# Splitting expert weights in one ScalarE copy and one GpSimd subtraction a block, with no VectorE mask

## The chip, the cores and the metric

The kernel runs on one core of one Trainium2 chip. The metric is device time in microseconds, the median of several executions. The engines are called PE (TensorE), DVE (VectorE), ACT (ScalarE), POOL (GpSimd) and SP (SyncE, which issues most DMAs here).

## The reference, cut to what matters

The input `x` has shape (32, 64, 1024). Two layers are run, each a conditioned chain of four small convolutions (same, upsample, same, downsample) followed by a feed-forward part, with a residual. The first layer's feed-forward part is a gated low-rank mixture of 64 experts:

```python
scores = xf @ Wr.T
top_vals, top_idx = jax.lax.top_k(scores, TOPK)        # 16 of 64
gates = jax.nn.softmax(top_vals, axis=-1)
G = jnp.zeros((N, K)).at[jnp.arange(N)[:, None], top_idx].set(gates)
h = jnp.einsum('nd,krd->nkr', xf, A)                   # 64 experts, rank 16, d = 1024
out = jnp.einsum('nkr,kdr->nd', h * G[:, :, None], B)
```

The second layer's is a product with int4 weights that are unpacked first. The change touches the preparation of `A` (with `Wr` in front of it) and `B` alone.

## The kernel before, in words

Samples are worked on in 16 pairs; a pair's tokens fill the 128 partitions. There are three phases, each a loop over the pairs: `layer0` (convolutions and the product with `[Wr | A]`, then gating, the result stored to DRAM), `layer0b` (that result transposed and multiplied by `B`, residual added), and `layer1` (convolutions and the unpacked weights).

Products with weights are made in float32r, in three parts. Each token tile is split into an upper half `th` and a lower half `tl` (scaled by RADIX = 4096), and a third tile `td` is the difference of the two. Each weight block of 128 rows has three planes to match: plane 0 is the upper half, plane 1 the remainder, plane 2 the crossed form, plane 0 − RADIX × plane 1. `product` runs all blocks with the planes 0 and 1 (`Q`) into one bank and plane 2 (`D`) into another. The blocks are `wa0` to `wa7` (1088 columns: 64 of `Wr`, 1024 of `A`) and `wb0` to `wb7` (1024 columns of `B`).

Making the planes is `split_weights`. Before the change it goes through a block in chunks of 512 columns (1088 gives 512, 512 and 64). For each chunk, `high` on DVE (line 150) clears the low 12 bits by two shifts, into a tile of the ring `hi`, which has three buffers and is shared with the splits of tokens (line 921) and with the unpacking of int4 weights (line 441). POOL subtracts that tile from the raw weights into plane 1 (line 383), and ACT copies it into plane 0 (line 384). Then DVE makes plane 2 for the whole block (`crossed_weights`, line 391).

While the blocks are still being split, the first two pairs (`WHOLE`) of `layer0` and of `layer0b` work on the raw weights in plain float32, without planes. Raw `A` blocks arrive by DMA in the rooms of later blocks: `w5` holds raw blocks 2 to 4, `w6` raw 5, 0 and 1, `w7` raw 6, and a tile named `kept` raw 7. So a block can be written only when the raw blocks that lie in its room have been read for the last time. Raw `B` blocks lie in the buffer `cv`; `wb0` to `wb7` take the rooms of `wa0` to `wa7`.

The code is written in program order, and a planner then orders the instructions of each engine by readiness and by its own estimate of times, so that an instruction can run well before its place in the text. `with tc.issue_after(ins)` sets a limit to that: each instruction that the block emits on the engine of `ins` is queued behind `ins`; instructions on other engines are not bound by it. The splits are spread over the start of `layer0` in this way: `wa3` before the loop (behind `done["c"]`, a PE instruction); `wa0` and `wa1` behind `xe` (a DVE instruction of `ends`); `wa4` behind `s2` (DVE); `wa2` behind `re` (an ACT copy); `wa5` and `wa6` during pair 1, `wa6`'s crossed form behind `lo`; `wa7` behind the gates of pair 1 (DVE), its crossed form behind `lo` too. `wb0` to `wb3` are emitted in pair 0 of `layer0b`, `wb4` to `wb7` in pair 1.

Beside the splits, in pair 0 of `layer0`, runs `ends(0, …)`: a row of small operations that make the outermost values of all samples, with PE matmuls `ye` (line 502), `ue` (521), `ve` (546) and `re` (559), and DVE work between them (`scaled`, lines 474 and 477, and `blur`, lines 530 to 532). Other names that come up: `rest` with the matmuls at 838, 847, 856 and 879 and the DVE additions 869, 870 and 887; the sums of composed weights on POOL (646, 652); second differences on POOL (726, 734); gating on POOL (1009); convolution matmuls 760, 761, 772, 777; the joining of products with the residual on DVE (1129, 1130); `tdx` and `tdh`, the tokens' difference on POOL (939).

Of the kernel before, what the change touches and what calls it, by code (L numbers as in the profile page):

```python
# [8 lines left out]
F32 = mybir.dt.float32  # L9
# [3 lines left out]
ALU = mybir.AluOpType  # L13
# [12 lines left out]
H = 512  # L26
# [37 lines left out]
def adaln_ffn_kernel(ctx: ExitStack, tc: tile.TileContext, t, out: bass.AP):  # L64
    nc = tc.nc
# [77 lines left out]
    def block(k, shape, dt, name):  # L143

        return wts.tile(shape, dt, tag=f"w{k}", name=name)

    def high(src, name):

        v = wk.tile([P, H], I32, tag="hi", name=name, bufs=3)[:, : src.shape[1]]
        nc.vector.tensor_scalar(  # L150
            v, src.bitcast(I32), BITS, BITS, ALU.logical_shift_right, ALU.logical_shift_left
        )
        return v.bitcast(F32)
# [222 lines left out]
    def split_weights(raw, w, ks, into, name, crossed=True):  # L376

        for k in ks:
            ws = block(k, [P, 3, w], F32R, f"{name}{k}")
            for c in range(0, w, H):  # L380
                cs = slice(c, min(c + H, w))
                h = high(raw[k][:, cs], f"{name}h{k}_{c}")
                nc.gpsimd.tensor_tensor(ws[:, 1, cs], raw[k][:, cs], h, ALU.subtract)
                nc.scalar.copy(ws[:, 0, cs], h)  # L384
            into[k] = ws
            if crossed:
                crossed_weights(into, k)

    def crossed_weights(into, k):
        ws = into[k]  # L390
        nc.vector.scalar_tensor_tensor(  # L391
            ws[:, 2], ws[:, 1], -RADIX, ws[:, 0], ALU.mult, ALU.add
        )
# [915 lines left out]
    def split_behind(v, k):  # L1309
        with tc.issue_after(done[v].ins):  # L1310
            split_weights(araw, AW, (k,), wa, "wa")
# [33 lines left out]
    with tc.issue_after(done["c"].ins):  # L1345
        split_weights(araw, AW, (3,), wa, "wa")
# [9 lines left out]
    for k in range(NP):  # L1356
# [31 lines left out]
        if k == 1:  # L1388
            beside[1] += [(split_weights, araw, AW, (5,), wa, "wa", False)]
            beside[2] += [(crossed_weights, wa, 5)]  # L1390
            beside[3] += [(weights, k + 2), (split_weights, araw, AW, (6,), wa, "wa", False)]
# [161 lines left out]
```

## Time and profile before

| | |
|---|---|
| median of 3 runs | 893.77 us (892.96 to 894.99) |
| the profiled execution | 891.84 us, span 889.8 us |
| mean granted clock of PE | 0.997 |
| line 150, masks of weights: 24 for `wa`, 16 for `wb` | 128x512 mean 0.56 us beside `araw`, 0.89 us beside `cv` |
| line 383, subtractions of the split | 128x512 mean 1.43 us (`wa`), 1.58 us (`wb`) |
| line 384, copies of the split | 128x512 mean 0.62 us |
| line 391, crossed form | 128x1088 mean 1.34 us, 128x1024 mean 1.97 us |

A profile is one execution; its times are microseconds from the start of the span. An instruction group is given as line, engine, operation, output and inputs, shape, count; what stands in brackets behind a piece of the timeline is how long the engine had been idle and what ended that. The chain of waits is followed back from the last instruction. In windows, the busy time of each engine in a stretch is followed by the granted clock of PE, the DMA share and GB/s.

### The profile page before, as it was taken

What the parts mean: (1) busy time and instruction counts of PE and PEld (TensorE: products, weight loads), DVE (VectorE), ACT (ScalarE), POOL (GpSimd) and SP (SyncE); (2) the same over time, 40 slices, a digit from 0 to 9 for tenths busy, and PEclk for the clock granted to TensorE, in tenths of its full rate; (3) what the DMA queues carried; (4) which work ended last, traced back from release to release, by engine and by line L of the source; (5) the groups of instructions that cost most, each with busy time, mean ns of one, the idle gap of its engine ahead of it and who ended that gap; (6) DMA issues with size and microseconds to landing.
All of it is one profiled execution on the core that took longest, in us unless ns stands there. A gap on an engine that the chain in (4) does not pass through costs nothing.

```text
span 889.8 us, 14891 instructions
## 1 busy us (share of the span) xinstructions
PE 861.4 (97%) x5023; PEld 773.3 (87%) x5023; DVE 723.9 (81%) x1461; ACT 355.6 (40%) x817; POOL 531.8 (60%) x745
## 2 busy tenths in 40 slices
PE   6989989999999999999999999999999999999997
PEld 5877789999999999994688888888899999999996
DVE  5565888888888888768996666669999999999996
ACT  6444444444444444433432221247333433443340
POOL 7335754666666665556572222343887888888884
PEclk9999999999999999999999999999999999999999
DMA  8531213222222222344465765566433234324311
GB/s 244 147 73 51 52 62 86 83 81 82 78 76 74 74 76 72 119 166 155 140 213 193 229 195 175 189 194 190 146 107 110 87 118 118 110 96 140 107 66 72
DMA packets 49739, 107.83 MB, mean 121 GB/s; under 512 B 13764, under 2 KB 22400, under 8 KB 49664
## 3 DMA queue, kind: packets, MB, share of 16 engines
q1 hardware_dynamic: 48704, 105.90, 37.9%
q10 hardware_dynamic: 960, 0.99, 0.5%
q8 instruction: 40, 0.66, 0.3%
q14 instruction: 35, 0.29, 0.1%
HBM read 69.00 MB, written 37.86 MB: 120 GB/s over the span
## 4 chain that ended last, share of the span: by engine, by line
PE 41%; DVE 8%; POOL 2%; issue 2%; ACT 0%; DVEq 0%; POOLq 0%
PE o L959 16%; PE q L1211 11%; PE f L623 3%; PE r L879 2%; PE c L777 2%; PE r L838 1%; PE ht L1085 1%; PE r L847 1%; PE c L772 1%; PE g L600 1%; DVE cv L720 1%; DVE cv L778 1%; DVE r L888 1%; DVE rt L870 1%; DVE nib L443 1%
## 5 line engine op out<-in xcount | busy, mean ns | idle before, releaser
L720 DVE TENSOR_TENSOR cv<-cv 128x257 f32<-128x257 f32 x120 | 106.7, 921 | 1.1 <-ACT cv L762 0.9
L734 POOL TENSOR_TENSOR cv<-cv 128x256 f32<-128x256 f32 x120 | 77.5, 646 | 28.8 <-DVE cv L720 15.9
L726 POOL TENSOR_TENSOR cv<-cv 128x128 f32<-128x128 f32 x100 | 38.8, 409 | 68.1 <-DVE su L1002 55.1
L1211 PE MATMUL q<-wq,thx 128*128 128x342 f32 x384 | 73.1, 332 | 3.5 <-ACT thx L917 2.9
L1211 PE MATMUL q<-wq,tlx 128*128 128x342 f32 x384 | 72.3, 330 | 0.0
L959 PE MATMUL h<-wa,tdx 128*128 128x352 f32 (+1 forms) x336 | 72.0, 350 | 0.2 <-DVE wa L391 0.2
L623 PE MATMUL f<-gs,iw 128*128 128x128 f32 (+1 forms) x384 | 68.2, 327 | 0.0
L623 PEld LDWEIGHTS f<-gs,iw 128*128 128x128 f32 x384 | 61.9, 191 | 5.5 <-POOL iw L260 0.2
L1211 PEld LDWEIGHTS q<-wq,thx 128*128 128x128 f32 x384 | 60.4, 189 | 5.5 <-ACT thx L917 4.0
L959 PE MATMUL h<-wa,thx 128*128 128x352 f32 (+1 forms) x336 | 64.8, 334 | 0.0
L774 ACT ACTIVATE yt<-c,be,al 128x257 f32<-128x257 f32 x56 | 31.7, 566 | 80.4 <-PE c L772 80.3
L879 PE MATMUL r<-cv 128*128 128x128 f32 x480 | 63.4, 275 | 0.0
L1211 PEld LDWEIGHTS q<-wq,tlx 128*128 128x128 f32 x384 | 61.6, 189 | 0.8
L959 PE MATMUL h<-wa,tlx 128*128 128x352 f32 (+1 forms) x336 | 62.3, 327 | 0.0
L959 PE MATMUL o<-wb,thh 128*128 128x512 f32 x224 | 59.8, 401 | 1.6 <-ACT wb L384 1.6
L939 POOL TENSOR_TENSOR tdx<-thx,tlx 128x1024 fp32r<-128x1024 f32 x14 | 35.4, 2532 | 43.0 <-ACT tlx L931 34.7
L959 PEld LDWEIGHTS h<-wa,tdx 128*128 128x128 f32 x336 | 56.8, 188 | 2.4 <-DVE wa L391 0.5
L879 PEld LDWEIGHTS r<-cv 128*128 128x128 f32 x480 | 58.4, 191 | 0.0
L646 POOL TENSOR_TENSOR cv<-cv 128x256 f32<-128x256 f32 x60 | 50.2, 836 | 13.2 <-ACT cv L641 13.1
L959 PE MATMUL o<-wb,tlh 128*128 128x512 f32 x224 | 58.0, 397 | 0.0
L638 ACT COPY cv<-f 128x256 f32<-128x256 f32 x64 | 23.9, 374 | 85.3 <-PE f L623 71.8
L980 ACT ACTIVATE hs<-h,outd 128x368 f32<-128x368 f32 (+1 forms) x42 | 23.7, 564 | 83.4 <-PE h L959 83.1
(318 smaller groups left out, 2266.9 us busy)
## 6 DMA issues: line engine op xcount, KB each, us to landing
cv<-in_x_dram SPq DMA_DIRECT2D x60, 256.0 KB
cv<-x1e SPq DMA_DIRECT2D x64, 192.5 KB
x1e<-dd SPq DMA_DIRECT2D x16, 514.0 KB
hgd<-hs SPq DMA_DIRECT2D x16, 512.0 KB
hg<-hgd SPq DMA_DIRECT2D x16, 512.0 KB
x1d<-x SPq DMA_DIRECT2D x16, 512.0 KB
xb<-x1d SPq DMA_DIRECT2D x16, 512.0 KB
out_dram<-o SPq DMA_DIRECT2D x15, 512.0 KB
```

Source lines behind the costliest of these rows:

```text
L623: done["f"] = nc.tensor.matmul(pv[:, n : n + 2 - k], iw[:, e].rearrange("p a b -> p (a b)"), v, start=(m == 0), stop=(m == len(steps) - 1) ...
L638: nc.scalar.copy(f8[:, 0::2], pv[:, :, h])
L646: nc.gpsimd.tensor_tensor(f[:, 4 * P : 6 * P].rearrange("p (a b) -> p a b", b=P), v[:, :, 0], v[:, :, 1], ALU.add,)
L720: nc.vector.tensor_tensor(d[:, k], yo[:, k : k + HQ], yb, ALU.subtract)
L726: nc.gpsimd.tensor_tensor(y[:, YB + k * P : YB + (k + 1) * P], y[:, 2 * k : 2 * k + 2 * P - 1 : 2], y[:, 1 : 2 * P : 2], ALU.subtract,)
L734: nc.gpsimd.tensor_tensor(e[:, :, k], d[:, :, 2 * k : 2 * k + HQ - 2 : 2], d[:, :, 1 : HQ - 1 : 2], ALU.subtract,)
L774: nc.scalar.activation(yt, mid, AF.Identity, bias=be0[:, n : n + 1], scale=a)
L879: done["r"] = nc.tensor.matmul(ps[:, j * P : (j + 1) * P], y[:, YE + (2 * q + k) * P : YE + (2 * q + k + 1) * P], w(q + 2 * k), start=True ...
L939: done["td"] = nc.gpsimd.tensor_tensor(*(v.rearrange("p a b -> p (a b)") for v in (td, *toks[key])), ALU.subtract)
L959: nc.tensor.matmul(banks[l == 2], toks[key][l][:, order(k)], w[:, cols], start=(k == first and l != 1), stop=(k == last and l in (2, min(n ...
L980: nc.scalar.activation(dst, qd[0], AF.Copy, scale=outd[:, 0, p : p + 1])
L1211: nc.tensor.matmul(ps, half[:, k], wq[at(k)][:, c * QC : (c + 1) * QC], start=(k == 0 and j == 0), stop=(k == NC - 1 and j == 1),)
```

## The change

The loop over chunks goes. ACT copies a whole raw block into plane 0, which is of the type float32r, in one operation; that copy rounds to the nearest value of the type, where the mask cut the low bits off. POOL subtracts plane 0, read as float32, from the raw block into plane 1, also in one operation a block. DVE's part in `split_weights` is the crossed form alone. The guards of the callers stand as they were.

```diff
         for k in ks:
             ws = block(k, [P, 3, w], F32R, f"{name}{k}")
-            for c in range(0, w, H):
-                cs = slice(c, min(c + H, w))
-                h = high(raw[k][:, cs], f"{name}h{k}_{c}")
-                nc.gpsimd.tensor_tensor(ws[:, 1, cs], raw[k][:, cs], h, ALU.subtract)
-                nc.scalar.copy(ws[:, 0, cs], h)
+            nc.scalar.copy(ws[:, 0], raw[k][:, :w])
+            nc.gpsimd.tensor_tensor(
+                ws[:, 1], raw[k][:, :w], ws[:, 0].bitcast(F32), ALU.subtract
+            )
             into[k] = ws
             if crossed:
                 crossed_weights(into, k)
```

## The prediction

> **What bounds the kernel now.** I read the page first. Its part 1:
>
> ```profile
> span 889.8 us, 14891 instructions
> ...
> PE 861.4 (97%) x5023; PEld 773.3 (87%) x5023; DVE 723.9 (81%) x1461; ACT 355.6 (40%) x817; POOL 531.8 (60%) x745
> ```
>
> TensorE (PE) is busy 97% of the span; only 889.8 − 861.4 = 28.4 us of it are gaps. Work taken off VectorE (DVE) is worth nothing unless it closes one of those gaps, so the second view is what PE waited for:
>
> ```profile
> PE ve L546 <- DVE room L532: 3.0, 1, 3.0
> ...
> PE c L777 <- DVE rt L870: 2.0, 3, 1.0
> PE o L959 <- ACT wb L384: 1.6, 2, 0.9
> ...
> PE c L777 <- DVE tlx L923: 1.0, 2, 0.6
> PE re L559 <- DVE room L532: 0.6, 1, 0.6
> ```
>
> The columns are total, times, longest. L384 is the split's own copy. Expert-weight splits run in two stretches only, 25 to 116 us (wa, factor A) and 383 to 436 us (wb, factor B). Inside those, the waits that touch the split are: 3.0 (L546), 0.6 (L559), 1.0 and 0.6 (L777, at 110.0 and 122.0 us; the third L777 wait is later), 0.2 (a crossed block of wa) and 1.6 (wb). Third view, the timeline at 41 to 50 us, shows what the 3.0 is:
>
> ```profile
> 41.17 0.93 PE L521 MATMUL ue<-room,cu 128*128 128x160 f32 x6
> ...
> 41.70 2.06 DVE L150 TENSOR_SCALAR wah<-araw 128x512 int32<-128x512 int32 x2 [1.38 <-ACT wa L384]
> ...
> 43.69 1.28 DVE L391 SCALAR_TENSOR_TENSOR wa<-wa 128x1088 fp32r<-128x1088 f32 x1
> ...
> 44.89 1.26 DVE L150 TENSOR_SCALAR wah<-araw 128x64 int32<-128x64 int32 x1
> ...
> 46.08 0.44 DVE L474 TENSOR_TENSOR room<-ue,alp 128x288 f32<-128x288 f32 x1
> ...
> 46.59 1.29 DVE L391 SCALAR_TENSOR_TENSOR wa<-wa 128x1088 fp32r<-128x1088 f32 x1
> ...
> 47.80 0.46 DVE L477 TENSOR_TENSOR room<-room,bep 128x288 f32<-128x288 f32 x1
> ...
> 49.55 0.73 PE L546 MATMUL ve<-room,cw 128*128 128x192 f32 x3 [3.01 <-DVE room L532]
> ```
>
> The bank `ue` is full at 42.1, but DVE reads it (L474) only at 46.08: masks (L150) and a crossed block (L391) stand in front, and a mask of 64 columns takes 1.26 because GpSimd (POOL) is subtracting beside it (shortest L150 here: 0.18). The whole row of small edge operations then ends late, and PE, out of other work at 46.54, waits. Fourth, the chain of waits in the wb stretch:
>
> ```profile
> 426.54 1.07 DVE x L1130
> 427.61 2.02 DVE wbh L150 x3
> 429.65 0.63 ACT wb L384
> 430.32 11.17 PE o L959 x41
> ```
>
> PE is held by a mask on DVE, that DVE reached only after L1130, and by the ACT copy behind it; ACT itself had been idle 7.19 us until 427.69. Fifth, the windows there (PE, PEld, DVE, ACT, POOL busy, then the granted clock):
>
> ```profile
> 429.00:430.00 1.00, 0.41 (x1) 0.09 (x1) 1.00 (x2) 0.72 (x2) 1.00 (x2) 1.00 0.52 184
> 430.00:431.00 1.00, 0.68 (x2) 0.58 (x3) 1.00 (x2) 0.27 (x1) 1.00 (x2) 0.67 0.48 127
> 431.00:432.00 1.00, 1.00 (x4) 0.81 (x3) 1.00 (x2) 0.94 (x4) 1.00 (x1) 0.50 0.95 385
> ```
>
> PE idles 0.73 + 0.59 + 0.32 = 1.64 us from 428 to 431, and right behind it the clock is 0.67, 0.50, 0.50, 0.63 for four microseconds, 1.70 us of full-speed work lost. The same matmul costs 3.32/8 = 0.415 us there and 1.98/8 = 0.248 at 435.9.
>
> **The change, part by part.** *Removed from DVE:* 40 masks (L150). wa: 14 of 512 columns busy 7.8, 7 of 64 columns 4.0, the three of `kept` 2.1; wb: 16 busy 13.5. Together 27.4 us, nearly all with PE busy beside it. *ACT:* 40 copies busy 9.5 + 1.9 + 9.4 = 20.8 become 16. The nearest row is L931, 128x1024 into fp32r at 1.056; with L384 (512: 0.616) the slope gives 1.11 for 1088. So 8×1.11 + 8×1.06 = 17.3. *POOL:* 40 subtractions busy about 50.5 become 16; nearest row L939, 128x1024 at 2.42 to 2.53, hence about 2.6 for 1088 and some 40 in all (quiet halves, 1.27 each, give the same per column: the saving is contention). *Crossed form:* 16 operations, unchanged.
>
> *The new wait.* POOL now waits for the ACT copy of the whole block, where it waited for a DVE mask of half a block. From raw block to crossed block: 1.11 + 2.6 + 1.28 = 5.0 us; before, undisturbed, 0.42 + 2×1.27 + 0.3 + 1.28 = 4.5. So 0.5 more per block, covered wherever blocks are made ahead of their use. Queued behind POOL's wait are the sums and differences (L646, L652, L734) and the gating (L1009).
>
> *What is let go.* `split_behind` and the `gates` guard hold back only instructions of the engine that the guard runs on. For wa0, wa1, wa4 and wa7 that engine is DVE; after the change only the crossed form is held (in wa7 nothing), and copy and subtraction may go as soon as the raw block has landed and the slot is free. The order by time shows that the planner pulls ready work forward (POOL memsets L483, emitted for pair 12, run at 434.66, during pair 1). In one-microsecond windows ACT shows 0.00 busy from 31 to 36 us and POOL 0.00 from 29 to 37 (its next subtraction starts at 37.57), so wa0, wa1 and wa4 can be split there: 3×2.6 = 7.8 of POOL's 9 idle us, from 28.5. The masks also leave the `hi` ring of three buffers, which they share with the token splits (L921): in the wb stretch wb4 to wb7 no longer queue there.
>
> *Gains, each by its gap.*
> 1. Edge chain, 42 to 50 us. L474 to L532 are 0.44+0.46+0.39+0.38+0.39 = 2.06; from 42.15 they end at about 44.3, and PE is busy until 46.54. If both crossed blocks (1.28 each) still fall among them, they end at 46.9 and some 0.5 of the wait stays; if an undivided subtraction (2.6) holds DVE there as well, at 49.5, and nothing is won. So 0 to 3.0, and 0 to 0.65 at L559, whose chain holds a mask too. Taken: 3.2 together, near the upper ends, since DVE is done with `xe` at 37.0 and waits for `ye` until 39.5, room for both crossed blocks before L474.
> 2. L777 at 110.0: 1.96 us of wa7 masks (106.85 to 108.8) stood before L869, whose bank was ready at 106.7; L869+L870 are 1.1, so they could end at 108.0, before PE comes at 109.0. All 1.0 goes. The 0.64 at 122.0 hangs on DVE's later backlog: 0 to 0.64. Taken: 1.0.
> 3. wb. Copies need only the raw block (the last is issued at 380.1) and a slot, free when pair 15 stops reading wa at about 395.5, and ACT has room (2.38 busy of 10 from 400 to 410). Bounds 0 (copies planned behind L1173 again) to 1.64 + 1.70 = 3.3. Taken 2.7: the chain's cause is removed, but POOL's eight blocks (8×2.5 = 20 us from 395, plus 3.4 of gating) end only around 420, a few us before PE needs them at 426.5.
>
> *Cost.* Unbroken POOL operations of 2.6 us in front of work PE waits for. PE already waited for POOL's sums (L838 behind L652) 0.9 us at 79.2 and 1.5 us at 132.7. Half a subtraction more (1.3) at one such place is −1.3; bounds 0 to 7.8 (three places). Taken 1.0.
>
> Sum: 3.2 + 1.0 + 2.7 − 1.0 = 5.9 us. Against the profiled execution (891.84 us, span 889.8) that is 885.9; the median of the runs stands 1.93 higher, 893.77, and by it 887.9.
>
> *A rule against the change.* Row first: the crossed operation that starts at 423.22, just after POOL began a 128x1024 subtraction (423.19, 2.34 us), took 3.40 us against 1.22 alone: 2.18 more, nearly all of the POOL operation. The Trainium skill, "SBUF — State Buffer" (section "SBUF: two separate sides"), says why: VectorE and GpSimd share one port pair, an exclusive lock for a whole instruction. By that rule undivided subtractions hold DVE up to twice as long per meeting: charged fully, 2.6 instead of 1.3 at each of the 16 blocks costs 16×1.3 = 20.8 us of DVE, still under the 27.4 that go. The sum above does not need this; the trace's DVE holds 6.9 us of such lengthening in the wb masks alone (13.5 − 16×0.41).
>
> **The rivals.** *Half of it.* One of the two larger gains fails: the edge chain stays late, or wb still waits. 893.77 − 2.7 or − 3.2: about 890.8. For it: the ends of 0 in terms 1 and 3.
>
> *Nothing reaches the end.* The gaps close, but PE meets another wait 20 us later. Against: windows 140 to 420 us show PE at 9.95 to 10.00 of 10, so what is gained before stays gained. 893.8.
>
> *Slower.* One mechanism: subtractions freed from their guards land on POOL ahead of the pair sums (L646, L652), between 60 and 132 us, where PE already waits for those sums. Each undivided one costs up to 2.6. With three of wa2, wa5, wa6, wa7 so placed, 7.8 is lost: 893.77 − 5.9 + 7.8 = 895.7, and 898.4 if wb gains nothing. It decides from two operations on (5.2 against 5.9), and loses clearly from three. For it: the guard on wa7 is gone, POOL is busy 8.6 of 10 from 100 to 110. Against: POOL's total falls by some 10 us, and the early blocks move into idle time.
>
> *The copy does not round.* The lower half would be zero and the output off; each instruction's time goes by shape, so the time would be the same as forecast.
>
> **How the numbers follow.** Forecast (gain of 4 to 9): 0.50. Half: 0.24. Nothing: 0.11. Slower: 0.15. Faster or slower by over 0.2% (1.8 us, about what a measurement of this kernel can tell from no change) then: faster 0.73, same 0.11, slower 0.16. The low end is all gaps closed at no cost, 3.0+0.65+1.66+0.2+3.34 = 8.9, thus 884.9, less 0.4 for the scatter of the runs (892.96 to 894.99): 884.5. The high end takes in half, nothing and the mildest of slower: 895.0. Outside lie about 0.04 below and 0.14 above. The likeliest case's own range is 885 to 890.
>
> **What would show it.** Right: no L546 wait near 46 us; L474 within 1 us of `ue`'s last matmul; POOL subtractions of 128x1088 between 28 and 40 us; all wb copies done before 426 us, no L959 wait for wb, and granted clock 1.00 from 428 to 436. Wrong: L838 waiting for L652 longer than 0.9 and 1.5 us, a wait of POOL for an ACT copy with the sums behind it, or PE waiting for L391 blocks of wa by more than the present 0.2 us. The wb gap filling again with a wait for tdh or for crossed blocks would fell the third term.

## The result, and the profile after

The changed kernel takes 904.67 us (904.22 to 905.43, 4 runs) against 894.1 us (892.96 to 894.99, 4 runs) for the kernel before: ratio 1.012, 95% interval 1.0105 to 1.0134. It is slower; the forecast was 887.9. In the changed code the lines behind the splits count one less than before (958 for 959, 1129 for 1130), and the split itself is 380 (ACT copy), 381 (POOL subtraction) and 390 (crossed form).

Part 1 of the page, after:

```profile
span 903.0 us, 14781 instructions
...
PE 869.2 (96%) x5023; PEld 780.0 (86%) x5023; DVE 708.4 (78%) x1421; ACT 351.5 (39%) x793; POOL 526.3 (58%) x721
```

DVE did lose its 40 instructions, but 15.5 us of work, not 27.4. PE runs the same 5023 instructions and is busy 7.8 us longer: part of the loss is PE at a lower clock, not PE waiting. What PE waited for, after (total, times, longest):

```profile
PE o L958 <- DVE x L1129: 6.9, 2, 5.8
...
PE r L837 <- POOL cv L651: 2.5, 2, 1.5
PE h L958 <- ACT hs L977: 2.2, 1, 2.2
PE cs L337 <- DVE room L340: 2.1, 1, 2.1
...
PE c L776 <- DVE rt L869: 1.0, 2, 0.7
```

The 3.0 us for `ve`, the 0.6 for `re` and the 1.6 for copies of wb are gone, and L776 waits for L869 twice instead of three times. Three new lines stand there: the join with the residual (L1129), the score evacuation (L977) and a small addition (L340). The timeline where the edge chain stood late before, now:

```profile
51.65 0.46 DVE L473 TENSOR_TENSOR room<-ue,alp 128x288 f32<-128x288 f32 x1 [1.42 <-PE ue L520]
...
53.37 0.39 DVE L531 SCALAR_TENSOR_TENSOR room<-room 128x224 f32<-128x224 f32 x1
...
53.91 1.21 PE L545 MATMUL ve<-room,cw 128*128 128x192 f32 x6
```

DVE now waits for `ue`, instead of `ue` for DVE, and `ve` follows without a wait: that gap has closed. So has the one in the wb stretch; the windows:

```profile
429.00:430.00 1.00, 1.00 (x3) 0.38 (x2) 1.00 (x2) 0.00 (x0) 0.00 (x0) 1.00 0.00 0
430.00:431.00 1.00, 1.00 (x4) 0.51 (x3) 1.00 (x2) 0.19 (x1) 0.17 (x1) 1.00 0.00 0
431.00:432.00 1.00, 1.00 (x4) 0.44 (x3) 1.00 (x3) 0.62 (x2) 0.03 (x1) 1.00 0.41 164
```

PE is full and the clock is 1.00. The time was lost elsewhere. To find where, I matched each PE matmul of the two traces and took the median difference of their starts (after minus before) for every 10 us of before:

| us of before | 10 | 20 | 30–40 | 50–90 | 100 | 120–390 | 400–420 | 430 | 440–600 | end |
|---|---|---|---|---|---|---|---|---|---|---|
| after, us late | 1.2 | 4.3 | 8.9 | 4.9 | 8.0 | 6.5 | 6.8 | 3.7 | 12.3 | 13.0 |

The steps down are the forecast gains (−4.0 at the edge chain, −1.5 behind 110, −3.1 at wb). The steps up are three new losses, 19.4 us together. The rest of the 13.0, 2.2 us, lies elsewhere: 1.2 ahead of the first split, 0.3 near 400 and 0.7 behind 600.

**Place 1, +7.7** (1.2 to 8.9)**.** The timeline after, and then the same addition before:

```profile
26.20 1.10 ACT L380 CAST wa<-araw 128x1088 fp32r<-128x1088 f32 x1
...
27.44 2.48 POOL L381 TENSOR_TENSOR wa<-araw,wa 128x1088 fp32r<-128x1088 f32 x1 [7.91 <-ACT wa L380]
27.46 2.50 DVE L340 TENSOR_TENSOR room<-room 128x32 f32<-128x32 f32 x1
...
30.02 1.49 PE L337 MATMUL cs<-room,cw 128*128 128x32 f32 x6 [2.08 <-DVE room L340]
```

```profile
25.04 0.42 DVE L150 TENSOR_SCALAR wah<-araw 128x512 int32<-128x512 int32 x1
25.37 0.19 DVE L340 TENSOR_TENSOR room<-room 128x32 f32<-128x32 f32 x1
...
25.59 2.94 POOL L383 TENSOR_TENSOR wa<-araw,wah 128x512 fp32r<-128x512 f32 x3 [6.41 <-DVE room L340]
```

`wa3`'s subtraction begins 0.02 us ahead of an addition of 32 columns, and the addition takes 2.50 us instead of 0.19, ending with the subtraction. Before, POOL's subtraction needed the mask (L150) that stood just ahead of L340 in DVE's own queue, and it began 0.03 us after L340 had ended. PE needs the sum for the second `cs` product and has no other work ready. The windows behind that (PE, PEld, DVE, ACT, POOL, then the clock):

```profile
28.00:30.00 2.00, 0.00 (x0) 0.00 (x0) 1.97 (x1) 0.38 (x1) 1.92 (x1) 0.99 0.66 42
30.00:32.00 2.00, 1.98 (x9) 1.98 (x10) 0.45 (x2) 0.00 (x0) 0.00 (x0) 0.50 0.04 9
...
38.00:40.00 2.00, 2.00 (x12) 2.00 (x11) 0.00 (x0) 1.69 (x2) 1.23 (x1) 0.50 0.77 156
40.00:42.00 2.00, 2.00 (x18) 2.00 (x18) 0.69 (x1) 0.00 (x0) 2.00 (x2) 0.95 0.01 2
```

From 30 to 40 us PE is full at clock 0.50: 5.0 us of full-speed work lost behind a wait of 2.1.

**Place 2, +3.1.** The timeline after at 106 to 111 us:

```profile
106.08 2.77 POOL L381 TENSOR_TENSOR wa<-araw,wa 128x1088 fp32r<-128x1088 f32 x1
...
108.88 1.10 ACT L380 CAST wa<-kept 128x1088 fp32r<-128x1088 f32 x1 [3.57 <-POOL wa L381]
109.88 1.46 ACT L977 ACTIVATE hs<-h,alp 128x352 f32<-128x352 f32 x3
...
110.48 1.26 PE L958 MATMUL h<-wa,thx 128*128 128x368 f32 x6 [2.19 <-ACT hs L977]
```

The copy of `wa7` writes the room in which raw block 6 lies, so it waits for `wa6`'s subtraction. The guard on `wa7` is an instruction of DVE and no longer binds the split, which has moved to ACT; the copy is queued ahead of the score evacuation, waits 3.57 us, and PE waits for the bank behind it. The clock is 0.50 from 112 to 114 and 0.67 to 116.

**Place 3, +8.6.** The timeline after, and the join before:

```profile
405.43 22.16 POOL L381 TENSOR_TENSOR wb<-cv,wb 128x1024 fp32r<-128x1024 f32 x7
...
408.83 16.55 DVE L390 SCALAR_TENSOR_TENSOR wb<-wb 128x1024 fp32r<-128x1024 f32 x5 [2.26 <-POOL wb L381]
...
425.30 1.06 DVE L1129 SCALAR_TENSOR_TENSOR x<-o,xres 128x512 f32<-128x512 f32 x1
...
433.19 0.78 SPq L1110 DMA_DIRECT2D xres<-in_x_dram  x1
...
441.23 1.03 DVE L1129 SCALAR_TENSOR_TENSOR x<-o,xres 128x512 f32<-128x512 f32 x1 [6.82 <-DMA xres<-in_x_dram]
...
442.37 0.47 ACTq L200 DMA_DIRECT2D cv<-in_cw_dram  x1
...
447.05 0.96 DVE L213 TENSOR_TENSOR cv<-cv 128x768 f32<-128x768 f32 x1 [4.79 <-DMA cv<-in_cw_dram]
...
449.25 1.03 DVE L1129 SCALAR_TENSOR_TENSOR x<-o,xres 128x512 f32<-128x512 f32 x1
...
450.33 3.44 PE L958 MATMUL o<-wb,tdh 128*128 128x512 f32 x8 [5.84 <-DVE x L1129]
```

```profile
411.20 1.96 DVE L1130 SCALAR_TENSOR_TENSOR x<-o,xres 128x512 f32<-128x512 f32 x2
...
415.57 0.83 SPq L1111 DMA_DIRECT2D xres<-in_x_dram  x1
```

With all copies made early, POOL subtracts seven blocks in a row, and the planner puts five crossed blocks in front of pair 0's join; each takes 3.3 us beside a subtraction (before, 1.23 alone and 1.97 in the mean). The join runs at 425.30 instead of 411.20. SP's stores of that result stand ahead of pair 1's residual load, which is issued at 433.19 (415.57 before); its first join ends at 442.3, the weights for the next layer (`cw`) are issued right then, DVE takes them (L213) ahead of the second join, and PE waits 5.8 us for that join's bank. The clock is 0.68 from 450 to 455. The chain of waits names the same link: L1129 at 449.33, then PE at 450.33.

### The profile page after: what moved, and what is told of

It reads as the page before. It is cut to its first block, busy times and chain, and to the rows that moved or that the text cites. A ratio compares the mean times of both kernels' runs of the same rounds, so it can differ in the third digit from the quotient of the medians.

```text
span 903.0 us, 14781 instructions
## 1 busy us (share of the span) xinstructions
PE 869.2 (96%) x5023; PEld 780.0 (86%) x5023; DVE 708.4 (78%) x1421; ACT 351.5 (39%) x793; POOL 526.3 (58%) x721
## 5 line engine op out<-in xcount | busy, mean ns | idle before, releaser
L958 PE MATMUL o<-wb,tdh 128*128 128x512 f32 x224 | 56.4, 401 | 7.0 <-DVE x L1129 6.9
L958 PEld LDWEIGHTS h<-wa,thx 128*128 128x128 f32 x336 | 54.9, 189 | 2.9 <-ACT hs L977 2.5
```

The source lines that it names most:

```text
L958: nc.tensor.matmul(banks[l == 2], toks[key][l][:, order(k)], w[:, cols], start=(k == first and l != 1), stop=(k == last and l in (2, min(n ...
```

## The experiments

My theory: the three places cause the loss, each because an instruction that PE's next work hangs on (an addition, an evacuation, a join) now stands beside or behind split work. A rival: the undivided subtraction is at fault by its length wherever it meets DVE. A second: one stretch alone (wa or wb) carries everything. Experiments 1 to 3 each move only the split's instructions, in one stretch; "late" is again the shift against before. The time given first is the median of the runs; shifts, waits and clocks are those of the one profiled execution.

**1. Copies of wa3, wa0, wa1, wa4 and wa2 on ACT behind the copy of `rows`, which follows the chain of L340.**

```diff
-        nc.scalar.copy(rows, ps[:B, :C])
+        done["rows"] = nc.scalar.copy(rows, ps[:B, :C])
...
     def split_behind(v, k):
+        with tc.issue_after(done["rows"].ins):
+            split_weights(araw, AW, (k,), wa, "wa", False)
         with tc.issue_after(done[v].ins):
-            split_weights(araw, AW, (k,), wa, "wa")
+            crossed_weights(wa, k)
...
-    with tc.issue_after(done["c"].ins):
+    with tc.issue_after(done["rows"].ins):
         split_weights(araw, AW, (3,), wa, "wa")
```

> The changed kernel, but the ACT copies of blocks wa3, wa4, wa0, wa1 (and wa2) are queued behind ACT's copy of the small tile rows; in the planned order one ACT copy (wa3) and two DVE instructions change places, all else is as in the changed kernel. Theory A (three collisions; here: POOL's undivided subtraction of wa3 holds the 128x32 addition L340 on DVE for 2.3 us, PE waits 2.1 us for it and then runs at half clock for 10 us): the wait of cs for L340 falls below 0.3 us, the clock stays 1.00 from 30 to 40 us, PE reaches ye at 38 to 39.5 us instead of 47.45, and the time falls by 8 to 9 us from 904.7 to about 896. Theory B (the work is dearer in its new form: undivided subtractions and copies, wherever they stand): the time stays within 2 us of 904.7. Theory C (the rounded weights themselves lower the clock): the clock stays 0.5 somewhere between 30 and 45 us and the time stays.

900.17 us, ratio 1.0054 (1.0032 to 1.0075). Timeline:

```profile
27.39 0.20 DVE L340 TENSOR_TENSOR room<-room 128x32 f32<-128x32 f32 x1
...
30.57 10.91 POOL L381 TENSOR_TENSOR wa<-araw,wa 128x1088 fp32r<-128x1088 f32 x4 [11.34 <-ACT wa L380]
...
31.55 4.07 DVE L596 TENSOR_SCALAR r<-w3p,al 128x128 f32<-128x128 f32 x2 [2.83 <-PE g L599]
```

The addition is short again, the wait for `cs` is gone, the clock stays at 1.00 from 24 to 50, and PE is 0.6 us early from 50 to 95, where it was 4.9 late. The weights are the rounded ones here too, so theory C, that these lower the clock, falls. The time falls by 4.5 us, half of the 8 to 9 expected. Four subtractions in a row now hold other DVE work (L596 takes 2 us each), and PE waits 1.2 us for `ye`; place 3 is dearer in the profiled execution (901.53 us, where the ten runs go from 894.65 to 901.55): its wait of 6.7 us is followed by 10.2 us at clock 0.50, where the changed kernel had 3.4.

**2. wa7's copy behind the score evacuation.**

```diff
-                nc.scalar.activation(dst, qd[0], AF.Copy, scale=alp[:, NL - 1, p : p + 1])
+                done["hs"] = nc.scalar.activation(
+                    dst, qd[0], AF.Copy, scale=alp[:, NL - 1, p : p + 1]
+                )
...
-            with tc.issue_after(done["gates"].ins):
+            with tc.issue_after(done["hs"].ins):
                 split_weights(araw, AW, (7,), wa, "wa", False)
```

> The changed kernel, but the split of wa7 is queued on ACT behind the last ACT evacuation hs of pair 1 (before the change the DVE gates held it there). Only wa7's ACT copy and POOL subtraction move. Theory A: PE's wait of 2.2 us for hs near 108 us goes, with the half clock behind it (112 to 115 us), so 2 to 3.5 us less: about 902. A wait for wa7's crossed block near 123 us may take up to 0.7 us of it. Theory B: no change beyond 1 us, 904.7. Theory C: half clock at 112 to 115 us stays.

901.44 us, ratio 1.0088 (1.0073 to 1.0103). Timeline:

```profile
108.20 0.55 ACT L977 ACTIVATE hs<-h,alp 128x368 f32<-128x368 f32 x1
108.65 1.09 ACT L380 CAST wa<-kept 128x1088 fp32r<-128x1088 f32 x1
```

The evacuation now stands ahead of the copy. No wait for L977 is left, and from 90 to 110 us the lateness falls by 0.5 instead of rising by 2.6. The time falls by 3.2 us, as expected.

**3. Crossed blocks of wb behind the joins of pair 0.**

```diff
+            joined_last = joined_last if p else done["joined"]
-            split_weights(braw, L, range(4 * p, 4 * p + 4), wb, "wb")
+            split_weights(braw, L, range(4 * p, 4 * p + 4), wb, "wb", False)
+            with tc.issue_after(joined_last.ins):
+                for j in range(4 * p, 4 * p + 4):
+                    crossed_weights(wb, j)
...
```

(`done["joined"]` is L1129; pair 0's first one bounds wb0 to wb3, its last one wb4 to wb7.)

> The changed kernel, but the eight crossed blocks of wb on DVE are queued behind joins: wb0 to wb3 behind the first join of pair 0 in the second phase, wb4 to wb7 behind the last. Theory A: the join L1129 (x<-o,xres) of pair 0 runs at about 418 us instead of 425.3, right after PE ends its banks; the residual of pair 2 is loaded earlier, PE's waits for the join (6.9 us in two places at 441 to 450 us) go, and the half clock behind them; 7 to 9 us less: about 896.5. Theory B: DVE still meets the undivided subtractions, the crossed blocks end later, and the tdh products wait for them: within 2 us of 904.7.

897.04 us, ratio 1.002 (1.0001 to 1.004). Timeline:

```profile
407.74 1.07 DVE L1129 SCALAR_TENSOR_TENSOR x<-o,xres 128x512 f32<-128x512 f32 x1 [8.54 <-PE o L958]
408.65 11.17 DVE L390 SCALAR_TENSOR_TENSOR wb<-wb 128x1024 fp32r<-128x1024 f32 x4
419.75 1.06 DVE L1129 SCALAR_TENSOR_TENSOR x<-o,xres 128x512 f32<-128x512 f32 x1
...
439.89 2.12 PE L958 MATMUL o<-wb,tdh 128*128 128x512 f32 x8 [0.74 <-DVE x L1129]
```

The crossed blocks are still slow (2.8 us each); what changed is their place. The step from 430 to 440 is 1.8 us instead of 8.6, PE's wait 0.7 instead of 5.8. The profiled execution is the fastest of ten (892.70 us), so these two may be on the low side; by the medians 7.6 us go, as expected, the most of the three.

**4. The changed kernel, with POOL's subtraction in pieces of 512 columns.**

```diff
-            nc.gpsimd.tensor_tensor(
-                ws[:, 1], raw[k][:, :w], ws[:, 0].bitcast(F32), ALU.subtract
-            )
+            for c in range(0, w, H):
+                cs = slice(c, min(c + H, w))
+                nc.gpsimd.tensor_tensor(
+                    ws[:, 1, cs], raw[k][:, cs], ws[:, 0, cs].bitcast(F32), ALU.subtract
+                )
```

> The changed kernel, but POOL subtracts in pieces of 512, 512 and 64 columns (wa) and 512, 512 (wb), behind the one ACT copy a block. Theory A: order matters, length less: L340 is held by one piece at most (0.2 to 1.3 us instead of 2.3), PE's gap near 28 us shrinks to under 1.2 us and the clock may stay up there, for 1 to 8 us; the other two places stay (3 and 8 us, the first because the copy of wa7 still waits for the last subtraction of wa6, the second because eight crossed blocks still stand ahead of the join): 896 to 904. Theory B (length of the lock is all): back to 894 or under.

905.7 us, ratio 1.0127 (1.0095 to 1.0159): no gain. Timeline:

```profile
26.98 1.29 DVE L340 TENSOR_TENSOR room<-room 128x32 f32<-128x32 f32 x1
...
28.32 0.85 PE L337 MATMUL cs<-room,cw 128*128 128x32 f32 x6 [0.87 <-DVE room L340]
```

The addition is held half as long, but clock 0.50 still follows the gap of 0.87 us, for 6.8 us, and places 2 and 3 stand (waits of 3.1 and 6.9 us). Theory B (894 or under) falls, and the 896 to 904 of theory A was missed as well: length alone is not the cause, and halving it is worth nothing here.

**5. Experiments 1, 2 and 3 together.**

> The changed kernel with the three orders of the first three experiments together. Theory A (three separate collisions, whose costs add): PE's progress against the kernel before is 0 to -1 us from 50 to 400 us (the two early stalls gone, the edge wait of 3.6 us gone too), about -4 at 430 and -2.5 to -3.5 at the end: about 891, faster than before by 2 to 4 us. Theory B (the new form is dearer wherever it stands): above 894.

889.11 us, ratio 0.9947 (0.9928 to 0.9967): faster than both kernels. From the waits:

```profile
PE ye L501 <- DVE room L493: 1.2, 1, 1.2
```

In the profiled execution, the fastest of nine (886.46 us), PE is early by 2.3 us from 50 on, 2.8 from 110, 6.2 at 430 and 5.1 at the end, and the mean granted clock is 1.000. Singly the three take 0.7, 0.3 and 1.0 points off the ratio, 2.0 in sum; together 1.7. They account for the whole loss (1.2) and give back part of the forecast gain. (The same three orders in the kernel before were not tried; the waits that they remove are not among its waits.) Of the split's waits there is left 1.2 us of `ye` for L493, held behind four subtractions.

**6. As 5, with wa0 and wa1 later, emitted beside wa2 behind `re`.**

```diff
-            split_behind("xe", 0)
-            split_behind("xe", 1)
...
-            beside[4] += [(split_behind, "re", 2)]
+            beside[4] += [(split_behind, "re", j) for j in range(3)]
```

(The copies of these three are then queued behind `re` as well.)

> As the version with all three orders, and the splits of wa0 and wa1 are queued on ACT behind re, where wa2's is, so that only two subtractions (wa3, wa4) run on POOL before the edge chain. Theory A (POOL's subtraction holds each DVE addition with two SBUF inputs that meets it): the 1.16 us wait of ye and the lengthened DVE operations at 31 to 41 us go (L596 4.07 us, L492 1.35 us in the first experiment); 1 to 3 us less than the version with all three orders: about 889. Theory B: the same as that version, or later splits make PE wait for wa blocks near 100 us, 1 to 3 us more.

892.56 us, ratio 0.9982 (0.9967 to 0.9996): slower than experiment 5. The wait for `ye` goes, as theory A said, but the time misses. Timeline:

```profile
69.64 2.48 POOL L381 TENSOR_TENSOR wa<-araw,wa 128x1088 fp32r<-128x1088 f32 x1
...
72.15 1.29 DVE L390 SCALAR_TENSOR_TENSOR wa<-wa 128x1088 fp32r<-128x1088 f32 x1 [3.92 <-POOL wa L381]
...
80.46 0.74 PE L837 MATMUL r<-cv 128*128 128x128 f32 x4 [4.03 <-POOL cv L651]
```

DVE stands idle 3.92 us at a crossed block whose subtraction is not done, with the choice of the top 16 queued behind it (L994, at 73.36, though its scores were out of the bank at 70.8). ACT's gate and copies, POOL's pair sums and PE's L837 follow late in turn. Clock 0.50 for 3.4 us follows the wait. The moved blocks had met another chain.

**7 and 8. The new form for one factor only, the old for the other.**

```diff
-            nc.scalar.copy(ws[:, 0], raw[k][:, :w])
-            nc.gpsimd.tensor_tensor(
-                ws[:, 1], raw[k][:, :w], ws[:, 0].bitcast(F32), ALU.subtract
-            )
+            if name == "wb":
+                nc.scalar.copy(ws[:, 0], raw[k][:, :w])
+                nc.gpsimd.tensor_tensor(
+                    ws[:, 1], raw[k][:, :w], ws[:, 0].bitcast(F32), ALU.subtract
+                )
+            else:
+                for c in range(0, w, H):
+                    cs = slice(c, min(c + H, w))
+                    h = high(raw[k][:, cs], f"{name}h{k}_{c}")
+                    nc.gpsimd.tensor_tensor(ws[:, 1, cs], raw[k][:, cs], h, ALU.subtract)
+                    nc.scalar.copy(ws[:, 0, cs], h)
```

(Experiment 8 has "wa" in the first line.)

> Blocks of wa as before the change, blocks of wb as after it. Theory A: PE's progress equals that of before up to 395 us, is 3 us ahead at 430 and 5 to 6 us behind from 445 us on, with the waits for the join: about 899.5. Theory B (each block is dearer by its own form): half of the 10.6 us, about 899.5 too, but spread over 395 to 435 us.

> Blocks of wa as after the change, blocks of wb as before it. Theory A: PE's progress is that of the changed kernel up to 395 us (about +5 at 50 to 95 us, +6.5 from 120 us; less where the half clock is shorter), then as before, with its own wb wait and half clock at 428 to 434 us; 898 to 901. Theory B: about 899.

For wb only: 901.17 us, ratio 1.0075 (1.005 to 1.01); the waits for the join (7.3 us) are there, those for L340 and L977 are not. For wa only: 898.01 us, ratio 1.0034 (1.0018 to 1.005); waits of 2.1 (L340) and 2.2 (L977), and wb's 1.6 as before. 0.75 and 0.34 points make 1.09 of the 1.2: each stretch carries its own loss. Experiment 7 also repeats the gap of before at `ve`: 3.00 us, from 46.85 to 49.85, where the kernel before had 3.01, from 46.54 to 49.55. The windows around it, in experiment 7 and then in the kernel before:

```profile
45.49:48.91 3.42, 1.36 (x12) 1.17 (x10) 3.32 (x6) 2.13 (x4) 1.24 (x2) 1.00 0.46 113
48.91:52.32 3.41, 2.47 (x8) 2.50 (x9) 0.93 (x4) 0.00 (x0) 0.00 (x0) 0.50 0.87 195
```

```profile
44.63:48.04 3.41, 1.91 (x17) 1.72 (x15) 3.34 (x5) 2.70 (x5) 1.79 (x2) 1.00 0.28 73
48.04:51.45 3.41, 1.90 (x14) 1.93 (x15) 1.91 (x6) 0.00 (x0) 0.00 (x0) 1.00 1.03 228
```

Behind the same wait of 3.0 us the clock is 0.50 for 6.8 us in one execution and 1.00 in the other. The windows are cut at the steps of a grid on which the clock changes; the next section works it out.

**9. As 5, with the subtraction in pieces of 512 (the edit of experiment 4).**

> As e5 (three reorderings, 889.1 us), with POOL's subtraction cut into pieces of 512 columns; the orders of the other engines are those of e5. Theory 'order, not length': once nothing critical stands beside the subtractions, their length matters only where four of them meet the edge chain at 29 to 40 us (L596 4.08 us for two, L492 1.35, PE waiting 1.2 for ye): that wait shrinks to under 0.6 and the time is 888 (886.5 to 889.5). Rival 'length': whole locks cost DVE time everywhere; DVE busy falls by over 10 us and the time is 886 or less. Rival 'more instructions cost': POOL's 24 further operations make the subtractions end later, the crossed blocks with them, and the time is 890 to 892.

886.96 us, ratio 0.9932 (0.9918 to 0.9945): the fastest version here, faster than both kernels. The wait for `ye` is gone, but 1.5 us for `ue` has come (a crossed block stands in front of the addition L476, there line 478); both profiled spans are 884.7, DVE's busy time falls by 3.9 us only, and the intervals of 5 and 9 overlap. With the order right, length decides little or nothing that these runs can tell apart.

**10. As 5, with wa0's and wa1's copies behind the position copy of pair 0.**

```diff
-        with tc.issue_after(done["rows"].ins):
+        with tc.issue_after(done["positions" if v == "xe" else "rows"].ins):
             split_weights(araw, AW, (k,), wa, "wa", False)
```

> As e5 (889.1 us), but the ACT copies of wa0 and wa1 (with them the two subtractions) are queued behind the position copy on ACT that follows in pair 0, so that two subtractions instead of four lie between 28 and 40 us and two at 46 to 51. Theory 'the four subtractions in a row are what makes ye late': L596 and L492 go back towards their lengths before, PE's 1.2-us wait for ye goes, the time is 887.5 (886 to 889). Rival 'the lock moves with them': the subtractions hold the small additions L476 and L529 to L531 at 45 to 50 us, PE waits 1 to 3 us for ve, and the time is 890 to 892, or more where the clock falls behind that wait.

890.35 us, ratio 0.9961 (0.9949 to 0.9974). The wait for `ye` goes, and two subtractions at 46 to 51 us take its place:

```profile
47.68 1.51 DVE L476 TENSOR_TENSOR room<-room,bep 128x192 f32<-128x192 f32 x1
49.11 3.57 DVE L390 SCALAR_TENSOR_TENSOR wa<-wa 128x1088 fp32r<-128x1088 f32 x1
```

L476 took 0.36 in the changed kernel; PE now waits 1.2 us for `re`. The lock moved with the blocks, as the rival said, though to `re` instead of `ve`. The intervals of 5 and 10 overlap, so the time alone does not tell them apart.

## Why the prediction was wrong, point by point

- **The three gains were right in place, and two of them near in size.** Edge chain: 4.0 us (3.2 taken). L777: the wait at 110.0 is gone, and 1.5 us came back behind 110 (1.0 taken); but where no wait for L977 stands ahead of it, in experiments 2 and 5, the step is 0.5 and 0.6, since PE there waits 0.5 us at L837, which it did not before. wb: 3.1 us with clock 1.00 from 428 to 436 (2.7 taken). Together 8.6 us in this trace.
- **The step that failed is the cost: 1.0 taken, 19.4 measured** (7.7 + 3.1 + 8.6). It looked only at POOL's pair sums, and these do not wait longer: 2.5 us in two waits, as 0.9 + 1.5 before. The bound of 7.8 was of that mechanism alone.
- **"What is let go" was read as gain only.** The paragraph saw that the guards on DVE bind nothing but the crossed form any more. It did not ask, for each freed copy, what lies behind it in ACT's queue (L977 behind `wa7`), nor, for wb's early copies, what the crossed blocks then stand in front of (the join, with SP's loads behind it). For `wa3` it saw nothing to let go: its guard is an instruction of PE and bound neither version. But the mask in DVE's queue had set when the subtraction began, as L340 ended, and that left with the mask. Experiments 1, 2 and 3 take the three away one by one.
- **The shared port was priced in total, not in place.** The row of 3.40 us at 423.22 was the right row, and the rule of the Trainium skill, "SBUF — State Buffer" (section "SBUF: two separate sides"), agrees with what came: L340 2.50 for 0.19, crossed blocks of wb 3.3 for 1.23 alone. DVE saved 15.5 us of the expected 27.4. Of the 11.9 that are missing, 6.6 are the eight crossed blocks of wb (22.4 us for 15.7) and 2.3 are L340. I set such lengthening against DVE's spare time, where it is cheap; the 2.3 us fell on the one addition that PE was waiting for.
- **A wait was priced at its length.** Behind the waits of 2.08 and 2.19 us lay 5.0 and, from 112 to 116, 1.7 us of lost clock. The prediction had counted such a loss (1.70) where it was to be gained, but none in its cost.
- **The rivals.** "Slower" had the side, not the mechanism: no pair sum was held by subtractions, in the changed kernel or in experiment 6. "Nothing reaches the end" had the mechanism of place 3 (a gap closes and PE meets another wait, said to be 20 us later, here some 15), but not its size. The argument against it, "what is gained before stays gained", holds from 120 to 390 us (6.5 throughout), for losses as well; it says nothing of 440, where the next layer's loads hang on the same join. No time here bears on whether the copy rounds.
- **The signs.** Those named for being right all came: no wait for `ve`, L473 at 51.65 right behind the last matmul of `ue`, subtractions at 34.05 and 38.77, the last copy of wb begun at 409.7, clock 1.00 from 428 to 436. They looked at the old gaps alone. Of those named for failure one was near: the wb stretch filling again with a wait for `tdh`, 15 us later than I looked.

**How much is lost clock, and why behind some gaps only.** In all twelve traces the clock changes on a grid of 3.41 us: the 19 stretches at half clock ahead of the last matmul last 3.41, 6.83 or 10.24 us, so that one costs up to 1.7, 3.4 or 5.1 us of full-speed work. In the changed kernel they come to 17.1 us, before to 3.4, in experiment 5 to none; so at most 6.8 of the 13.0 us are lost clock, and most of the rest is waiting. Where the grid lies differs from execution to execution. In the kernel before, the grid (carried back from the fall at 430.33) cuts the wait for `ve` at 48.04 into 1.50 and 1.51 us, and PE is busy for 56% of either piece; in experiment 7 2.06 us of it lie in one piece, PE is busy for 40% of that, and the clock falls as it ends. With every trace cut so, each piece at full clock in which PE was busy for 42% or less, 26 in number, is followed by half clock; of those with 54% or more only one is (69%, experiment 4); between the two both are found. So whether a gap of 1 to 3 us costs clock was in good part luck in each execution. Not settled: what makes a stretch one, two or three pieces long, and why the clock fell behind the 69%.

## What to carry to other kernels

When work moves from one engine to another, list for each moved instruction what paced it before (a guard, an operand, a place in a queue) and what it now stands ahead of; a guard binds one engine, and leaves with the instruction it bound. Price contention at the instruction that the next matmul needs, not in the engine's total, and add the lost clock to each new wait. If the change is slower but its own gaps have closed, put only the order right at the new waits: three such edits turned +1.2% into −0.5% here.

## What the runs showed of the hardware that I had not expected

- A subtraction on GpSimd holds even a tiny VectorE addition that meets it until it ends: 128x32 took 2.50 us beside a subtraction of 2.48, 1.29 beside one of half a block, 0.19 to 0.20 with POOL idle.
- Short gaps can halve PE's clock for long: 0.87 us (experiment 4, 6.8 us at 0.50) and 2.08 us (10.2 us at 0.50, with PE full). Yet 1.2 us (experiment 5) and, before, 3.0 us left it at 1.00, and the same 3.0 us halved it in experiment 7. The Trainium skill, "TensorE: Matmul & The Clock Gate" (section "Part 1: The HAM clock gate (the "warmup" mystery)"), gives about 3.4 us of idling before the clock halves and about 3.4 us of work before it returns, counted in free-running windows. The grid of 3.41 us, which lies differently in each execution, agrees with such windows; a fall behind a piece in which PE was busy for 40%, and 10.2 us at half clock with PE full, do not agree with the figures.
